# Four layer-0 passes of a two-image Mamba kernel issued as one pipeline of 64 blocks

## The chip, the cores and the metric

The kernel runs on one core of a Trainium2 chip. The core has five engines that run side by side: PE (matrix products), DVE (vector), ACT (pointwise functions), POOL (general) and SP, which here only issues transfers. The metric is the device time of one execution in microseconds; the time shown is the median of several executions. The profile is one more execution, recorded by the hardware profiler.

## The reference

Two images of 64x64 positions and 256 channels go through two residual layers. Each layer normalises its input over groups of 8 channels and adds what it computes to its input.

Layer 0 is a Mamba in four directions: rows and columns, each forward and flipped. Per sequence of 64 positions:

```python
xz = x @ in_proj_w.T                      # 256 -> 2 x 512
xi = silu(causal_conv(xi, 4 taps) + conv_b)
dt, Bm, Cm = split(xi @ x_proj_w.T)       # 16, 16, 16
dt = softplus(dt @ dt_w.T + dt_b)
h_t = exp(dt * A) * h_{t-1} + dt * xi * B_t        # 16 states per channel
y = sum_over_states(h_t * C_t) + xi * D
out = (y * silu(z)) @ out_w.T
```

Rows use the weights `mh`, columns the weights `mv`. The four results are joined and multiplied by `fc_w`, and `fc_b` is added.

Layer 1 runs four Mamba-2 calls (columns, rows, columns, rows) on its normalised input, each with an RMS norm, and adds the end to the layer's input. It is the same in both kernels but for one transfer.

## The kernel before

All data is fp32, with the channels on the 128 partitions. A whole image is held in the local memory twice: X, the input (tile name `XU`), and Y, layer 0's result. Layer 1 works in U, which takes X's place. `XU` and `Y` have one buffer each.

The outer loop goes over the images: load X, `layer0`, `layer1`, store. Inside `layer0` a loop goes over two passes: "h" (rows, weights `mh`), then "v" (columns, weights `mv`). A pass is 16 blocks of four sequences (256 positions), and both directions of a block run together as 512 columns.

A block's steps are methods of the class `Block`. Their order is not written as nested loops: `STEPS0` gives each step a due time in hundredths of a state, and every block lasts 3200 (two halves of the channels, u, times 16 states, n). `issue` (L174) sorts all steps of all blocks by `period * i + due time` and issues them in that order. Nearly all instructions are kept in it on their engine (`pin`); those without `pin` may be moved earlier. So the front of block i+1 (`norm_x`, `x_proj`, `conv`, `silus`, `bc_proj`, `dt_softplus`) stands between the states of blocks i and i-1, and its end (`y_back`, `gated`, `out_proj`, `residual`) among the states of block i+1. `norm_x` is due 5659 before a block's first state, `residual` 3969 after it.

Each state needs: the decays exp(dt·A) from ACT into PSUM tiles `ps_h` (`decay`, L311); the inflow dt·x·B, a 128x1024 product on POOL into a tile `b` for most states (`inflow`, L558) or products on PE for some; the scan over positions on DVE (`scan`, L577); the product with C on POOL or DVE (`times_c`, L588 and L591); and a sum over states on PE (`add`). The rows of B and C are spread over the partitions by transfers from DRAM, 256 KB each, one to two per state, all issued on SP (`bc_spread`, L475).

Ahead of its blocks each pass loads its weights on SP (L328 to L336, L354, L356), computes `neg_a` (ACT and DVE), builds 16 diagonal matrices of taps and 4 of the skip weight on POOL (`diag_w`, `diag_d`, L347 and L350), and multiplies `out_w` and `fc_w` into one matrix `w_out` on PE (L362). These weight tiles have one buffer each. Ahead of the first pass of an image `group_norm` (L254) takes 16 statistics on DVE and a square root on ACT, and layer 1 begins with another.

In layer 0 Y is written by the residual of pass h (projection plus bias plus X, L667) and added to by that of pass v (L677). X is last read by the `norm_x` of the last block of pass v. In `layer1` the last call adds U into Y block by block (L1102) and stores Y to the output on SP (L1103).

Of the kernel before, what the change touches and what calls it, by code (L numbers as in the profile page):

```python
# [8 lines left out]
F32 = mybir.dt.float32  # L9
AF = mybir.ActivationFunctionType  # L10
# [92 lines left out]

B_BY = ("GGGGTTGGGGTGGTGT", "GGGTGPGGGTGTGGTT")
# [69 lines left out]
def issue(blocks, period, steps):  # L174

    plan = [
        (period * i + step[0], i, n) for i in range(len(blocks)) for n, step in enumerate(steps)
    ]
    for _, i, n in sorted(plan):
        _, name, *args = steps[n]  # L180
        getattr(blocks[i], name)(*args)
# [101 lines left out]

def layer0(tc, k, d, X, Y):

# [6 lines left out]
    with ExitStack() as ctx:  # L292
        small = ctx.enter_context(tc.tile_pool(name="l0_small", bufs=2))
        wp = ctx.enter_context(tc.tile_pool(name="l0_w", bufs=1))
        one = ctx.enter_context(tc.tile_pool(name="l0_one", bufs=1))
# [26 lines left out]

        gscale, gshift = group_norm(nc, k, small, ps_mm, X)

        for axis, m, part in (("h", "mh", 2), ("v", "mv", 0)):

            w_in = wp.tile([P, KT, 2 * DI], F32, name="w_in")
            nc.sync.dma_start(out=w_in, in_=d[m + "_in_w"])  # L328
            w_x = wp.tile([P, CT, NX], F32, name="w_x")
            nc.sync.dma_start(out=w_x, in_=d[m + "_x_w"])  # L330
            w_dt = wp.tile([RANK, DI], F32, name="w_dt")
            nc.sync.dma_start(out=w_dt, in_=d[m + "_dt_w"])
            cols = wp.tile([P, CT, TAPS + 3 + NS0], F32, name="cols")
            nc.sync.dma_start(out=cols, in_=d[m + "_cols"])
            fcb = wp.tile([P, KT], F32, name="fcb")
            nc.sync.dma_start(out=fcb, in_=d["fc_b"])  # L336
            conv_w, conv_b = cols[:, :, 0:TAPS], cols[:, :, TAPS : TAPS + 1]
            dt_b, skip = cols[:, :, TAPS + 1 : TAPS + 2], cols[:, :, TAPS + 2 : TAPS + 3]

            neg_a = wp.tile([P, CT, NS0], F32, name="neg_a")  # L340
            act(neg_a, cols[:, :, TAPS + 3 :], AF.Exp)
            nc.vector.tensor_scalar(neg_a, neg_a, -1.0, -1e-30, ALU.mult, ALU.min)
            diag_w = wp.tile([P, CT, TAPS, P], F32, name="diag_w")
            diag_d = wp.tile([P, CT, P], F32, name="diag_d")
            for c in range(CT):
                for j in range(TAPS):
                    nc.gpsimd.tensor_scalar(  # L347
                        diag_w[:, c, j, :], k.ident, conv_w[:, c, j : j + 1], None, ALU.mult
                    )
                nc.gpsimd.tensor_scalar(diag_d[:, c, :], k.ident, skip[:, c, :], None, ALU.mult)  # L350


            out_w = three.tile([P, KT, DI], F32, name="b")
            nc.sync.dma_start(out=out_w, in_=d[m + "_out_w"])  # L354
            fc_w = three.tile([P, 2, KT, C], F32, name="b")
            nc.sync.dma_start(out=fc_w, in_=d["fc_w"][:, part : part + 2, :, :])  # L356
            w_out = wp.tile([P, CT, 2, C], F32, name="w_out")
            for c in range(CT):
                pw = ps_mm.tile([P, 512], F32, name="ps_mm")
                for j in range(2):  # L360
                    for kt in range(KT):
                        nc.tensor.matmul(  # L362
                            pw[:, j * C : (j + 1) * C],
                            lhsT=out_w[:, kt, c * P : (c + 1) * P],
                            rhs=fc_w[:, j, kt, :],
                            start=kt == 0,
                            stop=kt == KT - 1,
                        )
                act(w_out[:, c, :, :].rearrange("p j n -> p (j n)"), pw, AF.Copy)

            class Block:
# [3 lines left out]
                def __init__(self, i):  # L375
                    self.i = i
                    self.pp, self.pc, self.pd, self.dt, self.dtx = {}, {}, {}, {}, {}
                    self.h, self.b, self.prod, self.y, self.yg = {}, {}, {}, {}, {}
                    self.pt, self.scaled, self.yb = {}, {}, {}
                    self.sums = [0, 0]  # L380

                def norm_x(self):
                    xs = seq_view(X, axis, self.i)
                    self.xn = one.tile([P, KT, TB], F32, name="xn")
                    for kt in range(KT):
                        pin(
                            nc.gpsimd.tensor_scalar(
                                seqs(self.xn[:, kt, :]),
                                xs[:, kt, :, :],
                                gscale[:, kt : kt + 1],  # L390
                                gshift[:, kt : kt + 1],
                                ALU.mult,
                                ALU.add,
                            )
                        )


                def x_proj(self, pair):
                    self.pp[pair] = ps_mm.tile([P, 512], F32, name="ps_mm")
                    for j in range(2):  # L400
                        mt = 2 * pair + j
                        for kt in range(KT):
                            matmul(
                                self.pp[pair][:, j * TB : (j + 1) * TB],
                                w_in[:, kt, mt * P : (mt + 1) * P],
                                self.xn[:, kt, :],
                                kt == 0,
                                kt == KT - 1,
                            )

                def x_copy(self, pair):
                    if not hasattr(self, "xi"):
                        self.xi = one.tile([P, CT, TB], F32, name="xi")
                    if pair >= CT // 2 and not hasattr(self, "gate"):
                        self.gate = two.tile([P, CT, TB], F32, name="gate")
                    dst = self.xi if pair < CT // 2 else self.gate
                    half = dst[:, 2 * (pair % 2) : 2 * (pair % 2) + 2, :]
                    act(half.rearrange("p c t -> p (c t)"), self.pp[pair], AF.Copy)

                def conv(self, c, dr):  # L420
                    if dr == 0:
                        self.pc[c] = ps_mm.tile([P, V], F32, name="ps_mm")
                    ps = self.pc[c][:, dr * TB : (dr + 1) * TB]
                    xi = self.xi[:, c, ::-1] if dr else self.xi[:, c, :]
                    matmul(ps, diag_w[:, c, TAPS - 1, :], xi, True, False)
                    for j in range(1, TAPS):
                        matmul(
                            seqs(ps)[:, :, j:],
                            diag_w[:, c, TAPS - 1 - j, :],
                            seqs(xi)[:, :, : L - j],  # L430
                            False,
                            j == TAPS - 1,
                        )

                def conv_copy(self, c):
                    if not hasattr(self, "xc"):
                        self.xc = two.tile([P, CT, V], F32, name="xc")
                    act(self.xc[:, c, :], self.pc[c], AF.Identity, bias=conv_b[:, c, :])

                def silus(self):  # L440
                    act(self.xc, self.xc, AF.Silu)
                    act(self.gate, self.gate, AF.Silu)
                    pin(nc.scalar.preload_act_table_set(LOG_EXP))


                def bc_proj(self, part):
                    if part == 0:
                        self.px = ps_mm.tile([P, V], F32, name="ps_mm")
                    for c in (2 * part, 2 * part + 1):
                        matmul(  # L450
                            self.px[:NX, :], w_x[:, c, :], self.xc[:, c, :], c == 0, c == CT - 1
                        )

                def bc_spread(self):
                    self.dbc = one.tile([NX, V], F32, name="dbc")
                    act(self.dbc, self.px[:NX, :], AF.Copy)
                    rows = dram.tile([1, 2, NS0, V], F32, name="bc_rows")
                    nc.sync.dma_start(
                        out=rows.rearrange("o k n t -> (o k n) t"), in_=self.dbc[RANK:NX, :]
                    )  # L460
# [725 lines left out]
```

## Time and profile before

| what | us |
|---|---|
| median of 3 runs (8894.53 to 8904.46) | 8898.37 |
| the profiled execution | 8898.15 |
| its span, first to last instruction | 8895.4 |
| PE busy | 7993.0 (90%) |
| DVE busy | 7641.6 (86%) |
| ACT busy | 7032.3 (79%) |
| POOL busy | 7788.9 (88%) |

The stages by the trace (scan and product of layer 0 are L577 and L591, last add of layer 1 is L1102):

| stage | from | to |
|---|---|---|
| image 0, pass h, first scan to last product | 70.66 | 1604.41 |
| image 0, pass v | 1661.05 | 3190.63 |
| image 0, layer 1, to the last add into Y | 3190.63 | 4443.12 |
| image 1, pass h | 4514.97 | 6049.20 |
| image 1, pass v | 6106.30 | 7638.21 |
| image 1, layer 1, to the last add into Y | 7638.21 | 8891.52 |

A busy share over the whole span is a mean of stages with different limits: layer 1 is almost all PE, layer 0 almost all POOL and DVE. So the stages are read one by one. In a row of windows there stand: start and end, length, then the busy time of PE, of PE's weight loads, of DVE, ACT and POOL with their counts of instructions, the granted clock of PE, the share of the DMA engines and GB/s. In a row of waits: who waited for whom, microseconds in total, times, longest.

### The profile page before, as it was taken

The numbers are of one execution on the slowest core, as the hardware profiler recorded it, in microseconds if no ns is written. First come the engines' busy times: TensorE is split into PE (matmuls) and PEld (weight loads), VectorE is DVE, ScalarE is ACT, GpSimd is POOL, SyncE is SP. The second block draws the span as 40 slices with busy tenths as digits, with TensorE's granted clock in tenths as the row PEclk, the third lists the DMA queues.
The fourth block names the chain that finished last, engine by engine and source line by source line (L and its number), as shares of the span: only waits on it lengthen the run. The fifth ranks groups of instructions, "written<-read, shape, count | busy, mean of one in ns | idle before, by whom it ended". The sixth has DMA issues, their size and how long they took to land. (4 is left out here: it accounts for less than half of the span.)

```text
span 8895.4 us, 150537 instructions
## 1 busy us (share of the span) xinstructions
PE 7993.0 (90%) x55696; PEld 6624.0 (74%) x55696; DVE 7641.6 (86%) x7427; ACT 7032.3 (79%) x12078; POOL 7788.9 (88%) x4494
## 2 busy tenths in 40 slices
PE   8999998899899879999989999888999998799999
PEld 6777777677777767777767777776777777677777
DVE  7999999799999976766679999997999999767666
ACT  6888888688888867777768888886888888677776
POOL 7999999799999966666779999997999999666667
PEclk9999999899999989999989999999999999899999
DMA  4444444344444410000044444443444444200000
GB/s 136 148 146 149 148 149 147 113 147 148 147 146 149 146 61 9 1 9 4 25 133 148 148 146 148 149 144 113 147 148 147 145 149 146 61 9 1 9 3 19
DMA packets 524382, 943.06 MB, mean 106 GB/s; under 512 B 70976, under 2 KB 79680, under 8 KB 522112
## 3 DMA queue, kind: packets, MB, share of 16 engines
q1 hardware_dynamic: 523648, 933.44, 33.8%
q8 instruction: 440, 7.21, 0.3%
q14 instruction: 294, 2.41, 0.1%
HBM read 920.63 MB, written 12.58 MB: 105 GB/s over the span
## 5 line engine op out<-in xcount | busy, mean ns | idle before, releaser
L558 POOL TENSOR_TENSOR b<-dtx,b_row 128x1024 f32<-128x1024 f32 x1344 | 3162.4, 2375 | 2.2 <-DVE ps_h L577 2.2
L588 POOL TENSOR_TENSOR prod<-prod,c_row 128x1024 f32<-128x1024 f32 x1088 | 2566.9, 2372 | 58.0 <-DVE prod L577 56.3
L318 PE MATMUL ps_y<-ident,prod 128*128 128x128 f32 x16384 | 2154.0, 281 | 305.0 <-POOL prod L588 162.1
L318 PEld LDWEIGHTS ps_y<-ident,prod 128*128 128x128 f32 x16384 | 1897.7, 145 | 589.7 <-POOL prod L588 315.3
L577 DVE TENSOR_TENSOR_SCAN prod<-ps_h,b 128x1024 f32<-128x1024 f32 x960 | 2162.4, 2274 | 198.1 <-ACT ps_h L311 187.3
L311 ACT ACTIVATE ps_h<-dt,neg_a 128x512 f32<-128x512 f32 x2688 | 1847.1, 689 | 541.7 <-DVE prod L591 433.7
L577 DVE TENSOR_TENSOR_SCAN ps_h<-b,ps_h 128x1024 f32<-128x1024 f32 x576 | 1313.2, 2280 | 50.9 <-issue 31.6
L591 DVE TENSOR_TENSOR prod<-ps_h,c_row 128x1024 f32<-128x1024 f32 x960 | 1175.3, 1224 | 127.4 <-DVE ps_h L577 54.8
L311 ACT ACTIVATE scaled<-dtxt,bt 128x256 f32<-128x256 f32 x2560 | 1086.4, 495 | 219.4 <-PE ps_h L318 215.7
L715 PE MATMUL ps_mm<-xn,w_in 128*128 128x256 f32 x4608 | 1081.1, 385 | 26.7 <-DVE xn L842 26.7
L947 POOL TENSOR_TENSOR terms<-dta,within 128x512 f32<-128x512 f32 x512 | 523.4, 1044 | 586.1 <-DVE dta L915 572.8
L715 PEld LDWEIGHTS ps_mm<-xn,w_in 128*128 128x128 f32 x4608 | 875.7, 193 | 157.9 <-DVE xn L842 35.5
L318 PE MATMUL ps_h<-ident,scaled 128*128 128x128 f32 x5120 | 709.1, 283 | 262.8 <-DVE prod L577 245.9
L311 ACT ACTIVATE b<-dt,neg_a 128x512 f32<-128x512 f32 x1408 | 929.8, 707 | 0.0
L314 PE MATMUL ps_mm<-xi,diag_w 128*128 128x256 f32 (+3 forms) x4096 | 914.4, 374 | 0.0
L318 PEld LDWEIGHTS ps_h<-ident,scaled 128*128 128x128 f32 x5120 | 601.0, 146 | 419.0 <-ACT ps_h L311 321.0
L577 DVE TENSOR_TENSOR_SCAN ps_h<-ps_h,b 128x1024 f32<-128x1024 f32 x384 | 876.2, 2282 | 17.9 <-POOL b L558 10.9
L314 PEld LDWEIGHTS ps_mm<-xi,diag_w 128*128 128x128 f32 x4096 | 752.6, 190 | 78.4 <-ACT dtxt L311 0.2
L803 DVE SCALAR_TENSOR_TENSOR conv<-ps_mm,cols,conv 128x252 f32<-128x252 f32 (+2 forms) x1536 | 705.6, 473 | 72.1 <-ACT conv L712 35.8
L314 PE MATMUL ps_mm<-xn,w_in 128*128 128x256 f32 x2048 | 539.7, 412 | 2.4 <-ACT dt L311 1.7
L1054 DVE TENSOR_TENSOR yg<-ps_mm,gate 128x512 f32<-128x512 f32 x256 | 164.8, 685 | 407.8 <-PE ps_mm L715 407.8
L712 ACT ACTIVATE conv<-ps_mm,cols 128x256 f32<-128x256 f32 x512 | 261.4, 561 | 285.5 <-PE ps_mm L715 285.2
(137 smaller groups left out, 12215.8 us busy)
## 6 DMA issues: line engine op xcount, KB each, us to landing
c_row<-bc_rows SPq DMA_DIRECT2D x2048, 256.0 KB, 3.4
b_row<-bc_rows SPq DMA_DIRECT2D x1344, 256.0 KB, 3.3
XU<-in_x_dram SPq DMA_DIRECT2D x16, 512.0 KB, 8.1
out_dram<-Y SPq DMA_DIRECT2D x32, 256.0 KB, 2.4
w_in<-in_L_t_Win_dram SPq DMA_DIRECT2D x4, 1160.0 KB, 5.1
w_in<-in_L_b_Win_dram SPq DMA_DIRECT2D x4, 1160.0 KB, 7.6
bc_rows<-dbc SPq DMA_DIRECT2D x64, 64.0 KB, 3.0
w_in<-in_L_mh_in_w_dram SPq DMA_DIRECT2D x2, 1024.0 KB, 8.3
```

The source lines that it names most:

```text
L311: pin(nc.scalar.activation(*args, **kwargs))
L314: pin(nc.tensor.matmul(out, lhsT=lhsT, rhs=rhs, start=start, stop=stop))
L318: nc.tensor.matmul(out, lhsT=x, rhs=order, start=start, stop=stop, is_transpose=True)
L558: pin(nc.gpsimd.tensor_mul(b, self.dtx[u], self.row(u, 0, n)))
L577: nc.vector.tensor_tensor_scan(*(t.rearrange("p c t -> p (c t)") for t in (to, a, b)), 0.0, ALU.mult, ALU.add,)
L588: pin(nc.gpsimd.tensor_mul(prod, prod, self.row(u, 1, n)))
L591: pin(nc.vector.tensor_mul(prod, self.h[u, n], self.row(u, 1, n)))
L712: pin(nc.scalar.activation(*args, **kwargs))
L715: pin(nc.tensor.matmul(out, lhsT=lhsT, rhs=rhs, start=start, stop=stop))
L803: nc.vector.scalar_tensor_tensor(dsts[:, :, j:], pps[:, :, : L - j], w[:, TAPS - 1 - j : TAPS - j], dsts[:, :, j:], ALU.mult, ALU.add,)
L947: nc.gpsimd.tensor_mul(terms, self.dta[:, s, :].unsqueeze(2).to_broadcast([P, NH, L]), k.within.unsqueeze(1).to_broadcast([P, NH, L]),)
L1054: pin(nc.vector.tensor_mul(yg5[:, :, :, e, :], py, gate5[:, :, :, e, :]))
```

## The change

The loops over images and passes are taken out of layer 0. All four passes of 16 blocks go into one list of 64 blocks: image 0 rows, image 0 columns, image 1 rows, image 1 columns. A block takes its image and weights from two lists. What used to stand ahead of a pass or an image gets due times of its own, relative to the pass's first state, and is sorted into the same list:

- `WEIGHTS0`: the weights of passes 2 to 4 are loaded by transfers issued on ACT's queue, one by one, each after the last use of its single buffer in the pass before (`cols` and `neg_a` get two buffers). The diagonal matrices are built on POOL one at a time, and pinned.
- `IMAGE0`: image 1 is loaded in eight transfers on ACT's queue, due 8799 before its first state. Its statistics stand on DVE 75 apart; mean and variance follow. The square root and reciprocal are replaced by exp(-0.5 ln).
- The merged output weights of both kinds are computed once, at the start of the kernel (`MERGE_FIRST`, `MERGE_SECOND`), copied out of PSUM by DVE, kept in DRAM, and loaded for each pass (`load_out`). Before, they were computed in each of the four passes and copied by ACT.
- Y of image 0 is stored to DRAM (`spill`, eight transfers on ACT's queue, due 899 after image 1's first state); Y of image 1 takes its place in the local memory.
- Layer 1 then runs for image 1 first. As each block of its result is stored, the same part of image 0's Y is reloaded on SP's queue. Then layer 1 runs for image 0.

In the first pass X, weights and both merges' operands are loaded on SP, the group norm is issued at once, and the diagonal matrices follow the blocks' order, so that the first `norm_x` stands ahead of them on POOL. The steps of a block and their due times are unchanged.

```diff
+WEIGHTS0 = (
+    (-5497, "load_in"),
+    (-5386, "load_cols"),
+    (-4500, "decay_rates"),
+    (-4458, "diag_taps", 0, 0),
...
+    (-3540, "load_x"),
...
+    (-2612, "diag_taps", 3, 3),
+    (-2063, "load_dt"),
+    (-230, "diag_skip", 0),
...
+    (439, "diag_skip", 3),
+    (961, "load_out"),
+)
+IMAGE0 = (
+    (-8799, "load"),
+    (-7899, "stats", 0),
...
+    (-6774, "stats", 15),
+    (-6629, "moments"),
+    (-6554, "mean_sum"),
+    (-6479, "mean_dev"),
+    (-6404, "var_sum"),
+    (-6329, "factor"),
+    (-6254, "offset"),
+)
+SPILL = 899
+MERGE_FIRST, MERGE_SECOND = -1133, -555
...
+def plan(things, period, steps, first=0):
+    return [
+        (period * i + step[0], first + i, n, getattr(thing, step[1]), step[2:])
+        for i, thing in enumerate(things)
+        for n, step in enumerate(steps)
+    ]
...
+def issue(steps):
+    for _, _, _, do, args in sorted(steps, key=lambda step: step[:3]):
+        do(*args)
...
+            def load(self):
+                self.X = big.tile([P, KT, NTOK], F32, name="XU")
+                for j in range(NTOK // 512):
+                    t = slice(j * 512, (j + 1) * 512)
+                    queue = nc.scalar if self.b else nc.sync
+                    pin(queue.dma_start(out=self.X[:, :, t], in_=x[self.b][:, :, t]))
...
+            def factor(self):
+                log = small.tile([P, KT], F32, name="gn_log")
+                act(log, self.pv[:, 0:KT], AF.Ln, bias=k.eps_gn)
+                self.gscale = small.tile([P, KT], F32, name="gn_scale")
+                act(self.gscale, log, AF.Exp, scale=-0.5)
...
+            def spill(self):
+                self.kept = big_dram(tc, kept_ctx, [P, KT, NTOK], f"y_kept{self.b}")
+                for j in range(NTOK // 512):
+                    t = slice(j * 512, (j + 1) * 512)
+                    pin(nc.scalar.dma_start(out=self.kept[:, :, t], in_=self.Y[:, :, t]))
...
+                self.m, self.dma = m, nc.sync if first else nc.scalar
...
+            def load_out(self):
+                self.w_out = self.load(wp, [P, CT, 2 * C], "w_out", merged[self.m])
...
+                    w = two.tile([P, 2 * C], F32, name="w_merged", tag="yg")
+                    pin(nc.vector.tensor_copy(w, pw))
+                    pin(nc.scalar.dma_start(out=merged[self.m][:, c, :], in_=w))
...
+                self.i, self.axis = i % NBLK, "hv"[i // NBLK % 2]
+                self.image, self.w = images[i // (2 * NBLK)], weights[i // NBLK]
...
+        todo = plan([Block(i) for i in range(2 * n_img * NBLK)], period, steps)
+        todo += plan(weights[1:], period * NBLK, shifted(WEIGHTS0, period * NBLK), -8)
+        todo += plan(images[1:], 2 * period * NBLK, shifted(IMAGE0, 2 * period * NBLK), -4)
+        spill = [(2 * period * NBLK + SPILL, "spill")]
+        todo += plan(images[:-1], 2 * period * NBLK, spill, -4)
...
+        issue(todo)
+        return images[-1].Y, [image.kept for image in images[:-1]]
...
                         nc.sync.dma_start(out=out[:, :, t], in_=Y[:, :, t])
+                        if after is not None:
+                            nc.sync.dma_start(out=Y[:, :, t], in_=after[:, :, t])
...
-        layer0(tc, k, d0, X, Y)
-        U = big.tile([P, KT, NTOK], F32, name="XU")
-        layer1(tc, k, d1, U, Y, out[b])
+    with ExitStack() as kept_ctx:
+        Y, kept = layer0(tc, k, d0, big, d["x"], kept_ctx)
+        for b in reversed(range(out.shape[0])):
+            U = big.tile([P, KT, NTOK], F32, name="XU")
+            layer1(tc, k, d1, U, Y, out[b], kept[b - 1] if b else None)
```

## The prediction

> **What bounds the kernel now.** I read the slices first, for stages; then one window for each layer-0 pass and each place between passes; then the waits in a steady stretch; then the timeline of one seam.
>
> ```profile
> POOL 7999999799999966666779999997999999666667
> GB/s 136 148 146 149 148 149 147 113 147 148 147 146 149 146 61 9 1 9 4 25 133 148 148 146 148 149 144 113 147 148 147 145 149 146 61 9 1 9 3 19
> ```
>
> Per image: two layer-0 stretches with POOL at 9 and 148 GB/s, a notch between them (113 GB/s), then layer 1, where POOL is at 6 and almost nothing is moved. Next, windows (length, then busy time of PE, PEld, DVE, ACT, POOL):
>
> ```profile
> 70.66:1604.41 1533.75, 1366.22 (x8842) 1163.72 (x8840) 1474.56 (x906) 1285.93 (x2184) 1514.88 (x719) 0.95 0.47 147
> 1661.05:3190.63 1529.58, 1361.70 (x8842) 1158.85 (x8840) 1480.53 (x906) 1286.67 (x2184) 1508.45 (x697) 0.95 0.48 146
> 600.00:1360.00 760.00, 692.62 (x4521) 590.26 (x4519) 739.53 (x458) 652.76 (x1108) 755.98 (x354) 0.96 0.48 148
> 1604.41:1661.05 56.64, 49.22 (x216) 37.94 (x216) 2.49 (x9) 21.30 (x29) 6.59 (x6) 0.97 0.08 25
> 4443.12:4514.97 71.85, 47.25 (x167) 34.93 (x168) 12.94 (x26) 21.94 (x29) 19.83 (x29) 0.72 0.32 112
> ```
>
> Rows one and two are passes from first scan to last product; row three is steady. There POOL is busy 755.98 of 760 us (99.5%) and DVE 739.53 (97.3%): POOL sets the pace, DVE is right behind, ACT has 14% left. Rows four and five are a seam between the passes of an image and the start of image 1: POOL works 6.59 of 56.64 us and 19.83 of 71.85. The waits of POOL in the steady stretch say how tightly it follows DVE:
>
> ```profile
> POOL prod L588 <- DVE prod L577: 2.6, 4, 1.1
> POOL b L558 <- DVE ps_h L577: 0.3, 1, 0.3
> ```
>
> And DVE at the first seam (start, duration, instruction, idle before):
>
> ```profile
> 1603.19 1.22 DVE L591 TENSOR_TENSOR prod<-ps_h,c_row 128x1024 f32<-128x1024 f32 x1 [0.20 <-DVE ps_h L577]
> ...
> 1615.30 0.87 DVE L667 SCALAR_TENSOR_TENSOR Y<-ps_mm,fcb,XU 128x256 f32<-128x256 f32 x2 [6.67 <-PE ps_mm L314]
> 1661.05 2.29 DVE L577 TENSOR_TENSOR_SCAN prod<-ps_h,b 128x1024 f32<-128x1024 f32 x1 [44.88 <-ACT ps_h L311]
> ```
>
> The last product ends at 1604.41, the next scan starts at 1661.05: a block's projections, convolution and softplus run alone.
>
> **The books of before.** First scan 70.66; passes 1533.75 + 1529.58 + 1534.23 + 1531.90 = 6129.46; seams 56.64 and 57.1 (6049.20 to 6106.3); layer 1 of image 0 from last product to last add into Y 1252.5 (3190.63 to 4443.12); start of image 1 71.85; layer 1 of image 1 1253.3 (to 8891.52); last store 3.9. Sum 8895.4, the span. The median is 8898.37, so I add 3.0 at the end.
>
> **Part by part.**
> *Removed.* The two seams, 56.64 + 57.1. The start of image 1, 71.85. Image 0's drain, from last product 3190.63 to the last residual, 3201.51 + 1.30 = 3202.81: 12.2. Image 1's own drain stays. Together -197.8.
>
> *Front of the first block of a pass.* Its POOL work moves from the seam into the steady stretch: three inflows 6.96, dt times x 2.35, norm 1.5, memset 0.1, so 10.9 for each of three passes, 32.7. But a pass also has idle POOL time at its ramp and end: 1533.75 - 1514.88 = 18.9 against 0.5% (8) in steady work, so 10.9 are free and close up. I take 0. Without that cover it costs 32.7; if the second passes close up as far (1529.58 - 1508.45 = 21.1), it is a gain of some 8.
>
> *Diagonal matrices on POOL.* Before, the builds for the second pass already ran inside the first (the groups at 1536.46, 1541.68, 1545.74, 1550.95 and 1593.05: 2.93 + 1.77 + 2.94 + 1.78 + 2.35 = 11.8), while those of image 1 ran in its start. Three passes now have them in the stretch instead of two: +11.8.
>
> *Group norm of image 1.* 16 statistics of 0.685, two aggregates, some six small ones: 12.6 of DVE inside a stretch where DVE has 2.7% left. They are spread over 16.5 states of 3 us, so 1.3 fits in; POOL waits for the rest, as it follows DVE closely. Between 0 (POOL's work ahead covers all) and 11.3. I take 10, near the upper end. Ln and Exp take the place of the square root's table load; nothing.
>
> *Image 1 loaded from ACT's queue.* The load is due at 801 of block 29, where the norm of block 31 on POOL (741) has to have read X; on POOL that stands behind a product that needs a scan. ACT waits about one scan, one product, one norm: 2.28 + 2.37 + 1.4 = 6.0, and issues eight transfers at 0.74 (5.93 for eight on SP): 5.9. Behind it stand the decays of the next states. Two PSUM buffers give DVE one more state (3.5), so DVE is late by up to 8.5; POOL has two instructions in hand (4.7). Between 0 and 12; I take 6.
>
> The load also shares the DMA engines with the row broadcasts. In 4444 to 4458 the load of image 1 alone got 357 GB/s at a DMA share of 1.00; the rows need 148. If they go on undisturbed, the load takes 4.19 MB / (357 - 148) = 20 us, and the first statistics are due 9 states, 27 us, behind it. If the rows queue behind it, they stop for 4.19 MB / 357 = 11.7 us, which is the 12 above.
> The Trainium skill (DMA: Bandwidth & Descriptors, section Queues, rings and completion order) says that each engine takes turns packet by packet between the rows of different issuers. By that, as an estimate, the rows would lose a fraction of a microsecond each and this sum nothing; by a single ordered queue it would be 11.7. No row of this trace has two issuers at once.
>
> *Spill of Y.* Eight stores from ACT at 899, behind the residual (769): 5.9 of ACT with little wait, just ahead of softplus and its two table loads. DVE can cover 3.5. Between 0 and 12 (rows stopped, as above); 4. The first writer of Y in block 32 is its residual at 3969, 30 states or 90 us later, so it does not wait unless the stores take that long.
>
> *Weights.* Five single loads a pass from ACT, 0.33 to 0.76 each, 15 in all: 7 us of ACT, which is 14% idle. Each comes one or two states after the last use. Between 0 and 7; 3. The largest, w_in, has (5497 - 3614) / 100 = 19 states, 56 us, to land in; its kind took 8.3.
>
> *Start of the kernel.* Before, norm_x stood behind 20 diagonal builds on POOL (30.77); now it needs only the group norm, 21.95, so the projections are 8.8 earlier, less the convolution's waits for taps, 0. The first merge (32 matmuls, 7.07) falls where PE waited 4.0 for the SiLU: 3.1 later. The second merge stands before the next block's projection and dtx_back, whose ACT copies are ahead of the first decay: 7 more. With half a microsecond for table and queue: +2. Between -6 (the second merge hidden) and +6.
>
> *Layer 1 to layer 1.* The last block of Y has to be stored (2.4 to landing), then reloaded (256 KB, as a row: 3.4), with two waits of SP: +5.9. The layer's 16 statistics (3202.73 on, 9.6) come after the last residual before; now 14 of them can run while earlier pieces are in, if they move up as the diagonal builds did: -8.4. If not, 0. Queued behind SP's wait for a store is only the next store. Layer 1 itself is unchanged.
>
> **Sum.** -197.8 + 0 + 11.8 + 10 + 6 + 4 + 3 + 2 + 5.9 - 8.4 = -163.5. Span 8731.9, median 8735. The likeliest case's own range, with the small terms at half their spread: 8715 to 8760.
>
> **Rivals.**
> *The new work holds the seams open.* Image load and spill both stop the rows (+14 beyond what I took), the front is not covered (+32.7), the statistics do not move up (+8.4): 8790. For it: POOL is at 99.5%, so anything late is lost. Against: due times are many states apart. 8760 to 8890.
> *More is gained.* Load, spill and weights cost nothing (-13), the second passes close up (-8), the second merge hides (-8): 8706.
> *Slower.* One mechanism: POOL and DVE fall out of step. Four restarts begin each pass with the same lead; now nothing restores it. Place: the 17 products of a block that wait for a scan. Price: the gain is 163.5 over 64 blocks, 2.55 a block, so from 0.15 us more on each product it is slower than before; at 0.2, 64 x 17 x 0.2 = 218, 8953. For it: DVE has 2.7% left. Against: 4 such waits in eight blocks, 2.6 us in all, with no growth along a pass.
> *It does not overlap.* The loads into single-buffered tiles wait for the whole pass to end: the seams stay, about 8898. Against: in the trace the next pass's w_in was issued at 1428.7, 176 us before the last product.
>
> **How the numbers follow.** Forecast 0.70, more gained 0.09, seams held open 0.14, no overlap 0.01, slower 0.06. The range 8708 to 8785 holds the forecast, about half of the seams case and a third of the larger gain: some 0.8. A measurement of this kernel tells 0.2% (18 us) from no change. Faster 0.93, same 0.01, slower 0.06.
>
> **What would show it.** No DVE gap above 12 us between first and last scan; first scan near 73; 64 blocks in some 6164 us; POOL over 98% busy there. About 10 us of POOL waiting for DVE where the statistics run, and an ACT wait for POOL's norm before the image load. From the last add of the first layer 1 to the first projection of the second some 29 us (31.7 before behind layer 0, 3202.81 to 3234.47, with 5.9 added and 8.4 taken off). A block period of 98 us would make it wrong.

## The result and the profile after

| what | before | after |
|---|---|---|
| median in the same session, us | 8901.42 (4 runs) | 8781.7 (8779.02 to 8784.83, 4 runs) |
| ratio to before | | 0.9866, interval 0.9849 to 0.9883 |
| span of the profiled execution, us | 8895.4 | 8783.1 |

The kernel is 1.34% faster. The forecast was 8735 with a range up to 8785, so the time lies at the range's upper end: 120 us came where 163.5 were forecast. The slices of after, the rows shown of before:

```profile
POOL 7999999999999899999999999999676666667667
...
GB/s 154 149 146 146 148 150 146 151 148 147 146 148 147 151 160 148 146 149 148 148 150 147 146 149 148 145 148 148 75 7 4 9 1 25 31 9 1 9 4 18
```

Layer 0 is one stretch of 9s; of the notches only a single 8 is left, where image 1 takes over from image 0. Then come both layers 1. The windows of after, same columns as before (start and end, length, busy time of PE, PEld, DVE, ACT, POOL, clock, DMA share, GB/s):

```profile
72.90:6250.10 6177.20, 5547.61 (x35921) 4721.72 (x35919) 5936.68 (x3669) 5198.26 (x8813) 6074.71 (x2869) 0.95 0.50 148
600.00:1360.00 760.00, 691.53 (x4502) 589.44 (x4501) 736.08 (x457) 649.64 (x1101) 752.61 (x352) 0.96 0.50 148
...
2848.70:2971.00 122.30, 94.60 (x561) 80.51 (x562) 105.83 (x81) 82.58 (x140) 97.70 (x46) 0.86 0.57 154
3170.00:3279.50 109.50, 89.89 (x564) 77.12 (x564) 92.98 (x59) 81.25 (x138) 96.61 (x48) 0.89 0.58 177
6250.10:7539.40 1289.30, 1191.09 (x9780) 928.64 (x9780) 857.76 (x1882) 900.66 (x1613) 844.03 (x788) 0.95 0.04 13
7539.40:8779.20 1239.80, 1163.08 (x9732) 909.50 (x9732) 838.60 (x1847) 896.37 (x1609) 843.28 (x789) 0.96 0.03 10
```

Row one is the pipeline of 64 blocks, row two the steady stretch, rows three and four are blocks 29 and 32 (counted from 0, first scan to first scan; a block away from the seams takes 95.4), the last two are layer 1 of image 1 and of image 0. Against the prediction's books:

| stage | predicted | after | difference |
|---|---|---|---|
| first scan | 72.7 | 72.9 | +0.2 |
| 64 blocks | 6164 | 6177.2 | +13.2 |
| layer 1 of image 1 | 1252.5 | 1289.3 | +36.8 |
| layer 1 of image 0 | 1238.6 | 1239.8 | +1.2 |

So two places hold nearly the whole error: the change of image inside the pipeline, and the first layer 1. The places between passes cost what was forecast: blocks 14 to 16 take 101.4 + 99.4 + 97.2, which is 11.8 above three ordinary ones, blocks 46 to 48 take 11.2 above (predicted 11.8 for the diagonals and 1 for the weights).

**Inside the pipeline.** Waits of DVE from first to last scan (L760 is the scan in this kernel, L391 ACT's decays):

```profile
DVE ps_h L760 <- issue: 46.7, 39, 12.0
...
DVE prod L760 <- ACT ps_h L391: 18.3, 4, 12.8
```

The longest of each are the two gaps of the image change: 12.0 in block 29, where image 1 is loaded, 12.8 in block 32, where Y is stored. At the first, POOL's norm, ACT's eight issues (ACTq is the part of ACT that issues), its next instruction and POOL's next inflow read:

```profile
2875.30 1.52 POOL L570 TENSOR_SCALAR xn<-XU,gn_scale,gn_shift 128x256 f32<-128x256 f32 x2
...
2876.85 8.37 ACTq L418 DMA_DIRECT2D XU<-in_x_dram  x8
...
2885.27 1.71 ACT L391 ACTIVATE scaled<-dtxt,bt 128x256 f32<-128x256 f32 x4 [13.15 <-DMA XU<-in_x_dram]
...
2890.75 2.37 POOL L741 TENSOR_TENSOR b<-dtx,b_row 128x1024 f32<-128x1024 f32 x1 [9.32 <-DVE ps_h L760]
```

ACT stood 4.7 us until the norm ended (2876.82) and 8.4 us over the issues, 0.62 to 2.56 each; none of these followed the landing of a row. ACT's timeline at the second gap:

```profile
3195.30 1.40 ACT L391 ACTIVATE ps_h<-dt,neg_a 128x512 f32<-128x512 f32 x2
3196.07 0.62 ACTq L471 DMA_DIRECT2D y_kept<-Y  x1
3196.63 0.70 ACT L391 ACTIVATE b<-dt,neg_a 128x512 f32<-128x512 f32 x1
3197.00 0.56 ACTq L471 DMA_DIRECT2D y_kept<-Y  x1
3197.25 0.71 ACT L391 ACTIVATE b<-dt,neg_a 128x512 f32<-128x512 f32 x1
3202.03 9.58 ACTq L471 DMA_DIRECT2D y_kept<-Y  x6
3212.19 0.34 ACTq L481 DMA_DIRECT2D w_out<-w_out_mh  x1
3212.56 1.28 ACT L391 ACT_TABLE_LOAD   x1 [14.60 <-DMA y_kept<-Y]
```

The stores do not stand back to back. Each transfer names a semaphore among its operands, and ACT's transfers use the same eight as SP's. The last seven stores name it twice: as the one that their landing will raise, and as the one that they wait for. Set beside the moment when the transfer that last used the same semaphore landed, the issues read (worked out from the operands and the landing times of the trace):

```
store issued  semaphore  last landing on it   which was
3197.00       107        3196.98  (+0.02)     SP's b_row, issued 3193.57
3202.03       101        3202.01  (+0.02)     SP's c_row, issued 3196.32
3203.92       102        3203.90  (+0.02)     SP's c_row, issued 3198.21
3206.20       104        3206.18  (+0.02)     SP's c_row, issued 3201.61
3208.67       106        3208.65  (+0.02)     SP's b_row, issued 3203.92
3211.09       108        3211.07  (+0.02)     SP's c_row, issued 3204.34
```

Six of eight stores start 0.02 us after a row of SP's has landed. ACT stands in line for another queue's transfers, and the decays behind the stores come late. This fits the Trainium skill (Perfetto Trace Analysis, section DMA Instruction — HWDGE (DVE, Sync)): the reported start of such an instruction is the moment when all its semaphores are satisfied, so waiting shows as an idle engine and not as a long issue. The trace agrees: the store at 3202.03 is 0.52 us long, with 4.5 us between it and the store before.

**In layer 1.** The waits of DVE around the last call of layer 1 of image 1 (7250 to 7550), where Y's place is refilled piece by piece:

```profile
DVE gn_stats L336 <- DMA Y<-y_kept: 54.5, 7, 9.5
DVE yg L1269 <- PE ps_mm L930: 29.5, 9, 4.0
```

Statistics of the other image did move up, as the prediction hoped, but in front of their data. DVE stands idle ahead of them, up to 9.5 us at a time, and what is behind them on DVE waits too: from its first add into Y to its last this call took 266.1 us, where the kernel before took 238.5 (image 0).

That is 27.6 of the 36.8. The other 9.3 stand ahead of this call: from the last product of layer 0 to its first add 1023.2 us went by instead of 1014.0, with PE, busiest there, at work for 950.0 us instead of 940.0 and the granted clock at 0.95 instead of 0.96. In the twelve kernels below the same stretch took 1014.1 to 1021.7, and 1014.1 in two whose statistics had moved up too, so this part goes with the execution and not with the statistics.

### The profile page after: what moved, and what is told of

The parts are those of the page before. It is cut to its first block, busy times and chain, and to the rows that moved or that the text cites. A ratio compares the mean times of both kernels' runs of the same rounds, so it can differ in the third digit from the quotient of the medians.

```text
span 8783.1 us, 150445 instructions
## 1 busy us (share of the span) xinstructions
PE 7950.0 (91%) x55632; PEld 6598.0 (75%) x55632; DVE 7651.9 (87%) x7433; ACT 7016.0 (80%) x12062; POOL 7787.5 (89%) x4494
## 5 line engine op out<-in xcount | busy, mean ns | idle before, releaser
L771 POOL TENSOR_TENSOR prod<-prod,c_row 128x1024 f32<-128x1024 f32 x1088 | 2565.0, 2369 | 69.7 <-DVE prod L760 67.9
L391 ACT ACTIVATE ps_h<-dt,neg_a 128x512 f32<-128x512 f32 x2688 | 1847.6, 689 | 505.1 <-DVE prod L774 412.5
L760 DVE TENSOR_TENSOR_SCAN prod<-ps_h,b 128x1024 f32<-128x1024 f32 x960 | 2163.2, 2275 | 30.7 <-ACT ps_h L391 18.3
L760 DVE TENSOR_TENSOR_SCAN ps_h<-b,ps_h 128x1024 f32<-128x1024 f32 x576 | 1313.3, 2280 | 57.1 <-issue 34.7
L391 ACT ACTIVATE scaled<-dtxt,bt 128x256 f32<-128x256 f32 x2560 | 1086.5, 495 | 239.6 <-PE ps_h L398 223.5
L930 PE MATMUL ps_mm<-xn,w_in 128*128 128x256 f32 x4608 | 1094.6, 388 | 25.7 <-DVE xn L1057 25.7
L391 ACT ACTIVATE b<-dt,neg_a 128x512 f32<-128x512 f32 x1408 | 929.4, 707 | 0.0
L394 PE MATMUL ps_mm<-xi,diag_w 128*128 128x256 f32 (+3 forms) x4096 | 918.3, 374 | 11.9 <-ACT dt L391 11.8
L760 DVE TENSOR_TENSOR_SCAN ps_h<-ps_h,b 128x1024 f32<-128x1024 f32 x384 | 876.3, 2282 | 25.4 <-issue 12.0
L394 PE MATMUL ps_mm<-xn,w_in 128*128 128x256 f32 x2048 | 546.2, 415 | 4.7 <-POOL xn L570 4.2
```

The source lines that it names most:

```text
L391: pin(nc.scalar.activation(*args, **kwargs))
L394: pin(nc.tensor.matmul(out, lhsT=lhsT, rhs=rhs, start=start, stop=stop))
L760: nc.vector.tensor_tensor_scan(*(t.rearrange("p c t -> p (c t)") for t in (to, a, b)), 0.0, ALU.mult, ALU.add,)
L771: pin(nc.gpsimd.tensor_mul(prod, prod, self.row(u, 1, n)))
L930: pin(nc.tensor.matmul(out, lhsT=lhsT, rhs=rhs, start=start, stop=stop))
```

## The experiments

Twelve kernels. Block numbers and stages are from the profiled execution of each; times are medians with an interval of the ratio to the kernel before. Identical starts put the first scan at 72.3 to 78.4, and single runs of one kernel differ by 2 to 34 us, so stages are read before totals. The kernel before ran at 8898 to 8902 beside all of them. Some expectations call the engines by their full names: VectorE is DVE, ScalarE ACT, GpSimd POOL, SyncE SP.

**Statistics of layer 1 held behind the reload.**

```diff
-            nc.vector.bn_stats(stats[:, kt, j, :], src[:, kt, j * 512 : (j + 1) * 512])
+            pin(nc.vector.bn_stats(stats[:, kt, j, :], src[:, kt, j * 512 : (j + 1) * 512]))
```

> The 32 statistics of layer 1 (16 for each image) are kept in program order on DVE. Theory A: layer 1 of image 1 is 37 us longer than before (1289.3 against 1252.5) because 14 statistics of image 0 were moved up into its last call and hold DVE until the reload of Y lands (54.5 us of waits). Then it goes back to 1252 to 1254, the waits for the reload vanish from DVE but for one of some 6 us, and 8.4 come back because all statistics now follow the last reload: span 8783 - 37 + 8 = 8754. Rival B: stores and reloads on one queue slow the end of layer 1 by themselves. Then layer 1 of image 1 stays at 1285 or more, span 8780 or more.

Measured 8766.94 (ratio 0.9847, 0.9832 to 0.9862). Layer 1 of image 1 took 1259.6 instead of 1289.3, its last call 238.0; layer 1 of image 0 took 1249.1 instead of 1239.8. Both halves went the way of theory A, though the first stage stayed 6 above its 1252 to 1254. Of the 29.7 gained there 28.1 are the last call's, and 9.3 are lost in the next stage. A slow reload as such falls as a cause, since it is unchanged here. The last call tells the two apart in every profile: 262.9 to 266.1 in the eight kernels whose statistics had moved up, 237.9 to 238.5 in the five that hold them back or stage them. The median fell by 15, not by the 20 of these two stages; in the profiled execution the first scan came 4.4 later than in after.

**Load and spill in parts, 100 apart in the order.**

```diff
-        spill = [(2 * period * NBLK + SPILL, "spill")]
+        spill = [(2 * period * NBLK + SPILL + 100 * j, "spill", j) for j in range(8)]
```

and the same for the eight transfers of `load`.

> The eight transfers of the load of image 1, and the eight of the store of Y of image 0, are due 100 apart instead of together. Theory C: both cost time because ACT is held while it issues them in one lump (13.2 and 14.6 us without an activation, which makes DVE idle 12.0 and 12.8 us): its idle time shrinks to 1 to 3 us at each issue, block 32 goes from 109.5 to about 97 us and block 29 from 122.3 to about 113; span 8783 - 20 = 8763. Rival D, the bytes stop the row broadcasts: 175 GB/s more over 24 us still fit beside 148, so it expects about the same gain; this run says only what spreading is worth. If neither holds: 8778 or more.

Measured 8766.47 (0.9852, 0.9837 to 0.9867). Block 29 fell from 122.3 to 117.0, block 32 from 109.5 to 101.7, and DVE's longest wait for ACT there from 12.8 to 2.0. Blocks 29 to 32 together: 430.7 to 417.5. About 113 and 97 were expected for the two blocks, so spreading is worth less than theory C has it. With the transfers in one lump on ACT, block 29 took 121.3 to 122.4 in six profiles, block 32 107.4 to 110.7 in five (after's among them).

**One transfer each instead of eight.**

```diff
-                for j in range(NTOK // 512):
-                    t = slice(j * 512, (j + 1) * 512)
-                    pin(nc.scalar.dma_start(out=self.kept[:, :, t], in_=self.Y[:, :, t]))
+                pin(nc.scalar.dma_start(out=self.kept, in_=self.Y))
```

> The load of image 1 is one transfer of 4 MB instead of eight, and the store of Y of image 0 likewise. Theory C (ACT is held by issuing, each issue also waiting for an earlier transfer that uses the same semaphore): one issue each; ACT is held only for POOL's norm at the load (5 us) and next to nothing at the store; block 32 goes from 109.5 to 97 or less, block 29 from 122.3 to about 115; span 8783 - 18 = 8765. Rival D (4 MB in one burst keep the row broadcasts away): the burst is denser than before, DVE and POOL now wait for rows; block 32 stays at 108 or more, span 8783 or more.

Measured 8765.33 (0.985). Block 29 came as expected, 115.0. Block 32 did not: 107.1. ACT's timeline there, then DVE's waits:

```profile
3189.72 0.35 ACTq L469 DMA_DIRECT2D y_kept<-Y  x1
3190.28 1.32 ACT L391 ACTIVATE b<-dt,neg_a 128x512 f32<-128x512 f32 x2
3203.19 0.33 ACTq L479 DMA_DIRECT2D w_out<-w_out_mh  x1
3203.55 1.28 ACT L391 ACT_TABLE_LOAD   x1 [11.95 <-issue]
```

```profile
DVE prod L772 <- DMA c_row<-bc_rows: 5.9, 1, 5.9
DVE prod L758 <- ACT ps_h L391: 5.1, 2, 4.5
```

The store costs ACT 0.35 us, but the next transfer on ACT's queue, the load of `w_out`, starts only 0.07 us after the row that last used its semaphore had landed, and that row took 13.5 us from issue (median of such rows elsewhere in this run 3.55). The whole image in one transfer slows the rows, and through the shared semaphore ACT pays for it a second time.

**Diagonals built once, kept in DRAM, loaded for each pass.** The taps and skip matrices of both kinds are built by POOL at the start of the kernel and stored; every later pass has two loads on ACT's queue in place of 20 builds.

```diff
-    (-4458, "diag_taps", 0, 0),
...
-    (439, "diag_skip", 3),
+    (-4458, "load_taps"),
+    (-230, "load_skips"),
```

> The diagonal matrices of both kinds are built on POOL once, at the start, kept in DRAM and loaded for each later pass by two transfers on ACT's queue, in place of 20 builds a pass on POOL. If POOL sets the pace at the seams (forecast: 11.8 us a seam), the blocks beside the first and third seam (101.4, 99.4, 97.2 and 98.9, 101.0, 97.5) go back to 95 to 96, and some 9 us come off blocks 30 to 32: span 8783 - 33 = 8750, less up to 3 us more at the start. Rival: at the seams DVE or the weight loads on ACT set the pace and POOL's builds are hidden: the seam blocks stay at 98 to 101, span 8775 or more.

Measured 8758.43 (0.9836, 0.982 to 0.9853), 23 less than after. The first scan came at 86.8 in the profiled execution, 13.9 later than in after, where up to 3 were expected, and that execution, 8779.25, was the slowest of the four. In it the blocks at the third seam still took 98 to 99, though POOL was free in them. A block of the first seam, then blocks 45 and 47:

```profile
1516.00:1611.00 95.00, 85.45 (x564) 72.98 (x564) 92.24 (x59) 81.39 (x138) 94.84 (x45) 0.98 0.51 152
4424.20:4522.70 98.50, 91.41 (x564) 77.54 (x564) 92.53 (x59) 81.71 (x138) 94.56 (x45) 0.91 0.48 143
4621.90:4720.70 98.80, 91.51 (x564) 77.56 (x564) 92.51 (x59) 81.69 (x138) 94.83 (x45) 0.91 0.49 146
```

POOL is busy 94.6 to 94.8 in all three; what differs is the granted clock, 0.98 or 0.91, and with it PE's busy time. After has an ordinary block of the same kind, far from any seam:

```profile
738.50:837.00 98.50, 91.19 (x564) 77.56 (x564) 92.34 (x58) 81.71 (x138) 94.67 (x46) 0.91 0.48 144
837.00:931.20 94.20, 85.26 (x564) 72.87 (x564) 92.16 (x58) 81.39 (x138) 93.98 (x44) 0.98 0.49 149
```

So those 3 us go with the clock and not with POOL. The profiles of all fourteen kernels bear it out: of 512 blocks away from the seams, the 27 with a granted clock up to 0.92 lasted 97.7 to 99.0, the 86 with 0.97 or more 94.2 to 95.4. The price of the builds is read from another pair, below.

**Image 1's statistics taken at the start.** With the transfers spread as above, image 1 is brought once into Y's place at the start and its 16 statistics are taken there before block 0; later it is only loaded.

```diff
+        ahead = [(-1000 + i, "stats", i) for i in range(16)]
+        ahead += [(step[0] + 7800, *step[1:]) for step in IMAGE0[24:]]
+        todo += plan(images[1:], 0, ahead, -4)
```

> Load and spill transfers due 100 apart (as in the run with the transfers spread, 8766.5 us, pipeline 6166.3, block 29 117.0), and besides image 1 is brought once into Y's place at the start and its group-norm statistics are taken there before block 0; in the stretch it is only loaded, not measured. Theory (the 16 statistics, about 12.6 us of VectorE and 10 us of GpSimd waiting, are what is left of block 29's excess): block 29 104 to 107, pipeline 6153 to 6157, start lengthened by 0 to 3, time 8753 to 8758. Rival (block 29 waits for the order of work around the place that the load fills, the norm of block 31 and the free place, and the statistics run in time that is idle anyway): block 29 stays at 113 or more and the time at 8762 to 8770.

Measured 8764.08 (0.9847, 0.9833 to 0.986). Block 29's window and POOL's longest wait in it, first in the spread run:

```profile
2857.30:2974.30 117.00, 93.95 (x560) 78.83 (x561) 106.12 (x82) 82.65 (x140) 97.66 (x46) 0.91 0.58 161
```

```profile
POOL prod L778 <- DVE prod L767: 14.0, 9, 2.8
```

and then with the statistics gone as well:

```profile
2858.90:2961.20 102.30, 89.01 (x564) 75.18 (x564) 92.99 (x58) 81.48 (x138) 94.97 (x45) 0.95 0.60 179
```

```profile
POOL prod L784 <- DVE prod L773: 5.5, 5, 2.3
```

DVE's busy time falls by 13.1, POOL's wait for it by 8.5, the block by 14.7, blocks 29 to 32 by 10.3, the whole pipeline by 7.7. In block 29 the theory holds; the median moved by only 2.4 against the spread run, where the theory said 8 to 13, and its 8764 lies in the rival's range. Its profiled span, 8754.7, belongs to the low end of its timed runs (8756.38 to 8766.58), so how much of the block's gain reaches the median stays open.

**Layer 1's statistics staged behind the reload.** The two statistics of each 512 positions are pinned into the last residual loop, two to three blocks behind the reload of the piece; only the last piece's wait for the end.

```diff
+                            if self.i % 2 and self.i >= 3:
+                                j = (self.i - 3) // 2
+                                for kt in range(KT):
+                                    pin(nc.vector.bn_stats(st_next[:, kt, j, :], ...))
```

> Only layer 1 is changed: the statistics of the reloaded image are pinned, two to three blocks behind the reload of each 512 positions, in the last residual loop, the last chunk's at the end. Theory (the statistics that moved up ahead of their data held VectorE's queue, 54.5 us in one wait): last call of 16 blocks back to about 240 us from 266, layer 1 of image 1 1258 to 1264 (1289.3 after), layer 1 of image 0 1239 to 1242 (both gains at once, where pinning them all behind the reload gave up 9), time 8781.7 - 28 = 8750 to 8757, 9 below the run with them pinned (8766.9). Rival (the reload itself is late, and whoever reads it in that loop waits): VectorE waits for Y by the kept copy again, last call over 250, time 8765 or more.

Measured 8755.84 (0.9841, 0.9828 to 0.9855). Layer 1 of image 1 took 1257.6 and that of image 0 1242.4: both gains at once. In DVE's waits around the same call (7230 to 7520) the reload is gone from the head of the list, and waiting for PE, busiest in this stage, is back:

```profile
DVE yg L1268 <- PE ps_mm L929: 58.8, 16, 4.0
```

**Three edits together** (spread, statistics at the start, layer 1 staged).

> Spread transfers, image 1's statistics at the start, and layer 1's statistics staged behind the reload, together. If the three losses are separate: 8781.7 - 15 (spread) - 12 (statistics) - 28 (layer 1) = 8727, range 8718 to 8738. If GpSimd or the throttled clock takes back what one of them gives, 8745 or more.

Measured 8742.86 (0.9824, 0.981 to 0.9837): 39 below after, where 55 were expected of separate gains: between the ranges of both cases. The medians of the three alone had given 15.2, 2.4 and 25.9, 43.5 together, so most of the shortfall is what the early statistics failed to give alone; the profiled execution's first scan came 5.6 later than after's.

**These three and the diagonals from DRAM.**

> The three of the run before this, and the diagonals built once at the start, kept in DRAM and loaded for each pass. Theory (GpSimd's 35 us of builds at the seams are on the path): 8727 - 20 to 25 in the pipeline, + 10 to 14 at the start for the stores, 8712 to 8720. Rival, from the run with the diagonals alone (blocks with GpSimd free still took 98 to 99 us where the granted clock was 0.91, and the first scan came 14 us later): no gain beyond the run with three, 8725 to 8740.

Measured 8721.29 (0.9805, 0.9791 to 0.9818), 21.6 below the three, as the 23 of the edit alone. The pipeline went from 6161.2 to 6131.3, and the first scan from 78.5 to 84.6. The blocks at the seams:

```profile
1521.60:1616.60 95.00, 85.52 (x564) 72.99 (x564) 92.20 (x58) 81.39 (x138) 94.88 (x45) 0.98 0.49 151
...
4591.80:4687.00 95.20, 87.70 (x564) 75.11 (x564) 92.45 (x58) 81.39 (x138) 94.80 (x45) 0.95 0.49 151
```

Both blocks took 99.4 and 101.0 in after with POOL at 99.3 and 100.9. POOL's 35.4 us of builds are worth 30 in the pipeline, 25.7 of it in the ten blocks at the seams (the mean granted clock in the pipeline also rose from 0.956 to 0.960); 6 go back into the start. The time lies just above the theory's 8712 to 8720, by parts that were off: the three had measured 16 more than the 8727 it starts from, the pipeline gave more than 20 to 25, and the start cost less than 10 to 14.

**The spill from POOL's queue**, still eight stores in one burst.

```diff
-                    pin(nc.scalar.dma_start(out=self.kept[:, :, t], in_=self.Y[:, :, t]))
+                    pin(nc.gpsimd.dma_start(out=self.kept[:, :, t], in_=self.Y[:, :, t]))
```

> The eight stores of the spill are issued on GpSimd's queue instead of ScalarE's, still in one burst at the same due time. Theory (ScalarE's queue was held 14.6 us because each of its stores waited for a row transfer of SyncE with the same semaphore): ScalarE has no wait over 5 us there, VectorE's wait of 12.8 for the decays is 3 or less, block 32 is 100 to 104 (109.5 after), time 8772 to 8778. Rival (4 MB in a burst starve the rows): VectorE or GpSimd wait 5 us or more for c_row or b_row, block 32 106 to 109, time unchanged. Either way issuing may cost GpSimd up to 8 us of its own, which would show as GpSimd's gaps.

Measured 8769.51 (0.9855, 0.9842 to 0.9869). Block 32 took 102.5; ACT has no wait over 4 us there, and DVE none for the decays. POOL's timeline at the issues, then the block's window:

```profile
3210.67 5.82 POOL L471 DMA_DIRECT2D y_kept<-Y  x8
```

```profile
3176.80:3279.30 102.50, 87.92 (x564) 74.22 (x564) 93.08 (x59) 81.61 (x138) 102.35 (x56) 0.95 0.59 189
```

The same burst, on a queue that waits for no row of SP's, does without the 14.6 us on ACT and costs POOL 5.8 of issuing instead, for which DVE waits up to 4.4. Rows issued during the burst still took up to 7.1 us to land, and no engine waited for them. This is the run that tells held issues from starved rows: with eight parts it was the issues.

**Image 1's load two states later.**

```diff
-    (-8799, "load"),
+    (-8599, "load"),
```

> Image 1 is loaded two states later (due 8599 before its first state instead of 8799), nothing else. Theory (the load stands on ScalarE's queue before GpSimd has done the norm that reads the old image, and everything behind it waits): ScalarE's wait there goes, VectorE's gap of 12.0 falls to 4 to 8, block 29 117 to 119 (122.3 after), time 8776 to 8780. Rival (the eight issues themselves, 8.4 us, or statistics and builds make all of block 29's excess): block 29 121 or more, time 8780 to 8784.

Measured 8781.82 (0.9869): nothing gained, block 29 at 121.3, the rival's figures. ACT no longer waits for POOL's norm, yet it stands as long:

```profile
2882.53 1.32 ACTq L418 DMA_DIRECT2D XU<-in_x_dram  x2
2883.28 1.27 ACT L391 ACTIVATE dt<-ps_mm,cols 128x512 f32<-128x512 f32 x2
2884.06 0.55 ACTq L418 DMA_DIRECT2D XU<-in_x_dram  x1
2884.57 1.28 ACT L689 ACT_TABLE_LOAD   x1
2891.91 3.98 ACTq L418 DMA_DIRECT2D XU<-in_x_dram  x5
2896.00 1.42 ACT L391 ACTIVATE ps_h<-dt,neg_a 128x512 f32<-128x512 f32 x2 [10.15 <-DMA XU<-in_x_dram]
```

The norm is out of the way and ACT issues early, but five of the eight loads now start 0.02 us after a row's landing on their semaphore (2884.04, 2891.89, 2893.29, 2893.95, 2894.60). One wait took the other's place, so what the norm's wait costs by itself is not shown.

**One transfer each, and `w_out` loaded later.**

```diff
-    (961, "load_out"),
+    (1600, "load_out"),
```

> One transfer each for load and spill (as in the run with single transfers: 8765.3, block 32 107.1), and the load of w_out due 1600 after a pass's first state instead of 961, so that it no longer stands on ScalarE's queue in the middle of the 4 MB store. Theory (the w_out load was held 11.9 us by a row transfer that shares its semaphore): ScalarE's idle time of 11.9 us goes, block 32 100 to 103, time 8759 to 8762. Rival (the 4 MB store starves the rows whoever issues): VectorE still waits 5 us or more for c_row, block 32 104 to 107, time 8763 to 8767.

Measured 8759.77 (0.9845, 0.9831 to 0.9858). ACT's 11.9 us are gone and the time is as the theory said, but block 32 is 104.2, the rival's figure:

```profile
DVE prod L772 <- DMA c_row<-bc_rows: 7.3, 1, 7.3
```

With one 4 MB transfer both are real. Taking the held issue away gave 2.9 of block 32's 11.7; DVE waits for a row itself, and rows issued in the burst took up to 14.8 us to land (median elsewhere 3.4).

**All four edits, load four states later, spill 200 apart, stores of the early diagonals on SP's queue.**

> The run with all four edits (8721.3; block 29 102.4, block 32 100.1, first scan 84.6), and besides image 1 loaded four states later, the spill's stores 200 apart instead of 100, and the stores of the diagonals built ahead issued on SyncE's queue instead of ScalarE's. Theory (ScalarE waited 5.8 for the norm at the load, 4.4 for a row at the spill, and 10.8 and 5.8 for builds at the start): block 29 97 to 99, block 32 97 to 99, first scan 78 to 80, time 8708 to 8714. Rival (these waits are covered by others that end just behind them): 8717 to 8724.

Measured 8710.27 (0.9788, 0.9775 to 0.9801), the fastest of all: 71 below after, 188 below before. The total is as expected, its parts less so: block 32 is 95.5, an ordinary block, but block 29 stays at 101.5 and the first scan at 83.1, where 97 to 99 and 78 to 80 were expected. The granted clock in block 29 was 0.92, which by the blocks counted above goes with some 98 us; what holds up the rest of that block and the start is open.

## Why the prediction was right, and where it was off

The number was right with some luck. The time lies 3 us inside a range whose upper end was drawn to hold about half of the "seams held open" case; the likeliest case's own range, 8715 to 8760, was missed by 22 us.

- **Seams removed, front covered.** Right. Away from the seams a block takes 95.4, the three inflows, norm and product of a first block cost nothing that shows, and nothing stops between passes.
- **Diagonals +11.8.** Right. The forecast charged the difference between three passes of builds and the two that before already hid; all three are 35.4 us of POOL, and taking them out gave 26 to 30 in the pipeline.
- **Group norm of image 1, 10.** Right in place (POOL waiting for DVE) and in size by blocks 29 to 32 (10.3) and the pipeline (7.7). The medians (2.4) do not confirm the size.
- **Load 6 and spill 4.** The mechanism was ACT's queue, as stated; the size was off. Four ordinary blocks, 381.6, with 11.8 + 10 + 1 for the other terms make 404.4; blocks 29 to 32 took 430.7, so by subtraction load and spill cost 26.3. In the trace POOL stands idle 9.3 at the load and 9.0 at the spill, 18.3 where 10 were forecast. At the load the wait for POOL's norm was there as described (4.7, 6.0 forecast), but "issues eight transfers at 0.74" measured 8.4 instead of 5.9, and DVE covered 1.1 of ACT's 13.15, not 3.5. At the spill the step that failed is "5.9 of ACT with little wait": ACT stood 14.6, because six of the eight stores waited for rows of SP's. Spreading gave back 13.2.
- **Rows beside a transfer of ACT's.** The bounds were 0 and 11.7. In after, rows issued at the spill landed in 5.7 us (median of seven; 3.5 elsewhere), with one large transfer in 11.4 (of seven). So the estimate of a fraction of a microsecond a row was too small: it was 2.2 and 7.9. The prediction had drawn it from the turn-taking by packet in the Trainium skill (DMA: Bandwidth & Descriptors, section Queues, rings and completion order); whether the engines take turns that way, no run here shows.
- **Weights 3, start +2, reload +5.9.** Right: seams at 11.8 and 11.2; first scan at 72.9, though the first projection came only 6.6 earlier (24.8 against 31.4), not 8.8, and the same start gave 72.3 to 78.4 in eight profiles, so that the agreement within 0.2 is luck; 29.1 us from the last add of the first layer 1 (7539.4) to the first projection of the second (7568.56), 29 predicted.
- **"now 14 of them can run while earlier pieces are in, if they move up as the diagonal builds did: -8.4. If not, 0."** This is the step that failed. They moved up, and layer 1 of image 0 became shorter as forecast. But the step bounded the cost at 0, and the loss stood in the layer before, where DVE waited 54.5 us for pieces of Y: 27.6 of that stage's +36.8, and all of them returned when the statistics were held back or staged. The question of what is queued behind a waiting instruction was put for SP there, and not for DVE.
- **The rivals.** "Seams held open" named image load and spill, rightly, but with stopped rows as the cause, and listed the statistics with 8.4 for not moving; its 8790 lies near the result for partly wrong reasons. POOL and DVE did not fall out of step: a block takes 95.4, and the wait of POOL for DVE in the steady stretch is

```profile
POOL prod L771 <- DVE prod L760: 6.0, 5, 3.6
```

  in 760 us (2.6 before), and 67.9 us over the whole pipeline (56.3 over the four passes before). Of the signs named in advance, POOL's share (6074.71 of 6177.20, 98.3%) and the first scan came; no DVE gap above 12 did not, by 0.8.

## What to carry to other kernels

A transfer issued on a computing engine's queue is not only its issue time: ask which semaphore it will wait for and whose transfer used it last; in the burst of eight stores here six waited, so spread a burst, or issue it where nothing urgent stands behind. An instruction that is free to move up is a gain only if its data are there, since here all that stood behind it on DVE waited with it: place it a few steps behind the transfer. When work moves into a stretch bound by one engine, its price is nearly the full busy time on that engine (26 to 30 of 35 us here).

## What the runs showed of the hardware

- The start of a transfer on ACT's queue followed the landing of SP's transfer on the same semaphore by 0.02 us, eleven times in the two bursts shown (six stores of after, five of the loads due two states later), with ACT idle meanwhile for 14.6 and 10.15 us.
- Eight stores from POOL's queue took 5.82 us of POOL and were not held by SP's rows; they use eight semaphores of their own (111 to 118).
- With the same code at the start, the first scan came at 72.3 to 73.6 in five runs and at 77.1 to 78.4 in three; in the three the granted clock between 40 and 72 us was 0.89, in the five 0.95 to 1.00. That the clock is the cause is not shown.
- A block with the granted clock at 0.91 lasts 98.5 where one at 0.98 lasts 94 to 95, with POOL's busy time much the same. This falls on different blocks from run to run and can hide, or feign, a gain of a few microseconds at a seam.
